# A graph kernel's last unit: one-hot rows kept in its gather buffer, and its late sums shared between VectorE and GpSimd

## The chip, the cores and the metric

The kernel runs on one core of one Trainium2 chip. The metric is the device time of one execution in microseconds. An execution with the profiler on takes longer than one without; times without it are the metric, and the profile tells what happens inside.

## What is computed

The input is x (4096 nodes, 64 values each) and a 0/1 adjacency matrix of 4096 x 4096 with about 8 neighbours per row. Two layers follow one another, each with a layer norm and a ReLU ahead of it and a residual sum behind it. Cut to what matters:

```
# layer 0, on h = relu(layernorm(x)), curvature 1
w      = adj / max(adj.sum(1), 1e-8)
log_ij = logmap(h_i, h_j)                 # per edge: Mobius difference, arctanh of its norm
agg    = einsum('ij,ijc->ic', w, log_ij)
x      = x + expmap(0, agg @ weight0 + bias0)     # a tanh of the norm

# layer 1, on h = relu(layernorm(x))
support = h @ weight1
rank    = cumsum(adj != 0, axis=1);  deg = rank[:, -1];  k = min(deg, 100)
w       = (adj != 0) * where(rank - (deg - k) > 0, 0.5 ** (deg - rank), 0)
out     = x + w @ support + bias1
```

## The kernel before

Rows are handled in 32 blocks of 128. Four stages overlap in time.

**Load.** `load` reads the adjacency matrix (128 DMAs of 512 KB on SyncE's queue), TensorE transposes it (L888) and ScalarE writes it as one-byte floats to four resident arrays `masks[0..3]` (L891), eight row blocks each. TensorE packs the bits into words (L917), from which VectorE finds each row's neighbours (`search`, `tail_split`, `tail_first`, `tail_second`): up to six per row in a regular list (`ell`), and the rest of all rows in tails, three slots of 128 edges per row block.

**Units.** The edges of layer 0 are worked through in 17 units. Units 0 to 15 hold the regular lists of two row blocks (12 slots of 128 edges), and units 5 to 16 also the tails of two or three row blocks (up to nine slots). Unit 16, the last, has no regular list: it holds the tails of blocks 30 and 31, six slots. A unit goes through these steps:

- `fetch`: the unit's own rows come in by DMA on ScalarE's queue. For a tail this is `hr`, placed in the second half of a tile `mr` from the pool `blk`, which has one buffer; the first half becomes `mt`.
- `gather`: one indirect DMA per slot on GpSimd's queue (L1139) fills tile `g` (pool `gp`, two buffers; 21 slots of 65 floats per partition).
- `tail_rows`: ScalarE builds one-hot rows `oh` (L1156, L1163; one buffer in `blk`), TensorE transposes them into the one-bank pool `ps_m` (L1169), ScalarE copies them to `mt` (L1170), and TensorE picks the rows of `hr` with them (L1178): the first six slots into bank `sel` of `ps_s`, the others into `ps_m`.
- `differ` (L1192 to L1222): differences of gathered and own rows to tile `d`, and their squares back into `g`; `weigh` (L1234 to L1251): the weight of each edge, small VectorE and ScalarE operations.
- `total`: the regular list is added up on VectorE. For the tail ScalarE scales the one-hot rows to `mr` (L1261), TensorE adds up by destination into a bank `sel` of `ps_s` (L1266), and `total_tail` adds that to `y` (L1295).

`d`, `w`, `oh` and `mr` have one buffer each, so these steps of one unit follow those of the unit before.

**Groups.** `middle` ends layer 0 and begins layer 1 for five groups of row blocks (8, 8, 8, 6 and 2). It has four stages: scale and subtract (L1323 to L1330), transposes and the product with weight 0 (L1302, L1345), tanh and layer norm on VectorE and ScalarE (L1353 to L1359, L698 to L711), and transposes and the product with weight 1 (L1386, L1390), whose result is split in three bf16 parts in `sup` (L1403). Group 3 (six blocks) needs units up to 15, group 4 (two blocks) needs unit 16.

**Sums.** `w @ support` is taken in four sums over source blocks: sum 0 has the 16 blocks of groups 0 and 1, sum 1 the seven that follow and belong to group 2, sum 2 six of group 3 and sum 3 three of group 4. Each sum is taken for 4 arrays p and 4 pairs n of row blocks, by `collect(c, p, n)`: 2 x (blocks) matmuls of 128x192 (L1422, with L1430 for the last source in sum 3) into one of the two banks of `ps_a`, and then the three parts are added into `acc`. There are two ways to do this:

- VectorE: one reduction out of the bank to `wsb` (L1441) and one multiply-add into `acc` (L1445);
- GpSimd, by way of ScalarE: a scaled copy to a tile of the right size (L1436) and three adds into `acc` (L1438). The tile is `mr` of `blk` for even n and `dg` of `lst` for odd n; each has one buffer.

Before, sums 1 and 2 take the second way always, sum 3 for n of 2 and 3, sum 0 never: 40 collects by GpSimd, 24 by VectorE. After each second collect of an array's last sum, `write` sends four row blocks out.

**The order of the work.** Each step is entered in a plan with a due time, written out by hand as `at(time, step, ...)` (L1456 and on). Steps are issued in the order of due times, and a priority is made of the due time, 30 us less for the steps named in EARLY (`fetch`, `gather`, `tail_rows`, `differ`, `weigh`, `total`, `middle` and the list steps, but not `collect`). A planner then fixes one order of instructions for each engine, and on the chip each engine runs its order, waiting at each instruction. A tile whose buffer is in use waits until all users of the buffer are done.

At the end a flag (L1559 to L1565) decides whether a general path is needed (L1567 to L1569); with these inputs it is not.

Of the kernel before, what the change touches and what calls it, by code (L numbers as in the profile page):

```python
# [11 lines left out]
F32 = mybir.dt.float32  # L12
BF16 = mybir.dt.bfloat16
# [6 lines left out]
P = 128  # L20
# [36 lines left out]
TB = 3  # L57
MAXT = 3
# [490 lines left out]
def kernel(  # L549
# [34 lines left out]
    nc = tc.nc  # L584
# [4 lines left out]
    DT = D + 1  # L589
# [4 lines left out]
    NSL = 2 * ELL + MAXT * TB  # L594
# [14 lines left out]
    hp_d = dram.tile([P, NB, 3 * DT], BF16, name="hp_d")  # L609
# [6 lines left out]
    with ExitStack() as fast:  # L616
# [174 lines left out]
        late = masks[NQ - 1].bitcast(F32).rearrange("p b c -> p (b c)")  # L791
# [39 lines left out]
        gp = fast.enter_context(tc.tile_pool(name="gp", bufs=2))  # L831
# [24 lines left out]
        for c, (_, nb, _) in enumerate(sums):  # L856
            n = nb + (c == len(sums) - 1)
# [254 lines left out]
        def fetch(u):  # L1112
            rb = u["ell"]
            if rb is not None:
                hi = blk2.tile([P, 2, DT], F32, name="hi")
                u["hi"] = hi[:, :, 1:DT]
                nc.scalar.dma_start(out=hi, in_=tab_v[:, rb : rb + 2, :])
            if u["tail"]:
                t0, nt = u["tail"]

                u["mr"] = blk.tile([P, MAXT * TB, P], F32, name="mr")
                half = u["mr"].rearrange("p b c -> p (b c)").bitcast(BF16)
                u["mt"] = half[:, 0 : MAXT * TB * P].rearrange("p (b c) -> p b c", c=P)
                hr = half[:, MAXT * TB * P :][:, 0 : MAXT * 3 * DT]
                u["hr"] = hr = hr.rearrange("p (b c) -> p b c", c=3 * DT)
                nc.scalar.dma_start(out=hr[:, 0:nt, :], in_=hp_d[:, t0 : t0 + nt, :])

        def gather(u):
            rb = u["ell"]
            g = u["g"] = gp.tile([P, NSL, DT], F32, name="g")  # L1130
            idx = []
            if rb is not None:
                idx = [ell_i[:, rb + b, s : s + 1] for b in range(2) for s in range(ELL)]
            u["e2"] = len(idx)
            if u["tail"]:
                t0, nt = u["tail"]
                idx += [tail_i[:, t0 + b, t : t + 1] for b in range(nt) for t in range(TB)]
            for k, i in enumerate(idx):
                nc.gpsimd.indirect_dma_start(  # L1139
                    out=g[:, k, :],  # L1140
                    out_offset=None,
                    in_=tab_d,
                    in_offset=bass.IndirectOffsetOnAxis(ap=i, axis=0),
                )
            u["ns"] = len(idx)

        def tail_rows(u):

            if not u["tail"]:
                return  # L1150
            t0, nt = u["tail"]
            nb = nt * TB
            oh = u["oh"] = blk.tile([P, MAXT * TB, P], BF16, name="oh")

            for k in range(nb):
                nc.scalar.activation(  # L1156
                    oh[:, k, :],
                    row128,
                    AF.Abs,
                    bias=tail_r[:, t0 + k // TB, k % TB : k % TB + 1],  # L1160
                    scale=-1.0,
                )
            nc.scalar.activation(oh[:, 0:nb], oh[:, 0:nb], AF.Relu, bias=1.0, scale=-1.0)  # L1163
            mt, u["sel"] = u["mt"], []
            for k0 in range(0, nb, SEL):
                part = range(k0, min(k0 + SEL, nb))
                mp = ps_m.tile([P, SEL, P], BF16, name="mi")
                for k in part:
                    nc.tensor.transpose(mp[:, k - k0, :], oh[:, k, :], ident_b)  # L1169
                nc.scalar.copy(mt[:, k0 : part.stop], mp[:, 0 : len(part)])  # L1170
            for k0 in range(0, nb, SEL):
                part = range(k0, min(k0 + SEL, nb))
                pool, name = (ps_m, "mi") if k0 else (ps_s, "sel")
                sel = pool.tile([P, SEL, DT], F32, name=name)
                u["sel"].append((k0, part.stop, sel))
                for k in part:
                    for n in range(3):
                        nc.tensor.matmul(  # L1178
                            sel[:, k - k0, :],
                            lhsT=mt[:, k, :],  # L1180
                            rhs=u["hr"][:, k // TB, n * DT : n * DT + DT],
                            start=(n == 0),
                            stop=(n == 2),
                        )
# [68 lines left out]
        def total(u):  # L1253

            d, rb, ns, r = (u[k] for k in ("d", "ell", "ns", "r"))
            e2 = u["e2"]
            if u["tail"]:
                t0, nt = u["tail"]
                mr = u["mr"]
                for k in range(nt * TB):  # L1260
                    nc.scalar.activation(  # L1261
                        mr[:, k, :], u["oh"][:, k, :], AF.Copy, scale=r[:, e2 + k : e2 + k + 1]
                    )
                ag = u["ag"] = ps_s.tile([P, SEL, DT], F32, name="sel")
                for k in range(nt * TB):
                    nc.tensor.matmul(  # L1266
                        ag[:, k // TB, :], lhsT=mr[:, k, :], rhs=d[:, e2 + k, :],
                        start=(k % TB == 0), stop=(k % TB == TB - 1),
                    )
            if not e2:  # L1270
                return
            q, b = divmod(rb, QB)
            if b == 0:
                st["y", q] = yp.tile([P, QB, DT], F32, name="y")

            re = r[:, 0:e2]
            nc.vector.scalar_tensor_tensor(
                re, ell_v[:, rb : rb + 2].rearrange("p b s -> p (b s)"), 0.0, re,
                ALU.is_gt, ALU.mult,
            )  # L1280
            nc.vector.tensor_tensor(d[:, 0:e2], d[:, 0:e2], cols(re, DT), ALU.mult)
            sv = d[:, 0:e2].rearrange("p (b s) c -> p b s c", b=2)
            for dst, one, two in (
                (sv[:, :, 0:3], sv[:, :, 0:3], sv[:, :, 3:6]),
                (sv[:, :, 0:1], sv[:, :, 0:1], sv[:, :, 1:2]),
                (st["y", q][:, b : b + 2, :].unsqueeze(2), sv[:, :, 0:1], sv[:, :, 2:3]),
            ):
                nc.vector.tensor_tensor(dst, one, two, ALU.add)
# [124 lines left out]

        def collect(c, p, n):

            pool = 0 < c < len(sums) - 1 or (c == len(sums) - 1 and n >= 2)
            b0, nb, _ = sums[c]
            end = c == len(sums) - 1
            o = ps_a.tile([P, 2, 2 * P], F32, name="a_ps")
            for k in range(2):  # L1420
                for j in range(nb):
                    nc.tensor.matmul(  # L1422
                        o[:, k, 0:W3],
                        lhsT=masks[p][:, b0 + j, bass.ts(2 * n + k, P)],
                        rhs=sup[c][:, j, :],
                        start=(j == 0),
                        stop=(j == nb - 1 and not end),
                    )
                if end:
                    nc.tensor.matmul(  # L1430
                        o[:, k, 0:W3], lhsT=last, rhs=sup[c][:, nb, :], start=False, stop=True
                    )
            ab = acc[:, p * QB + 2 * n : p * QB + 2 * n + 2, :]
            if pool:
                ev = (lst if n % 2 else blk).tile([P, 2, W3], F32, name="dg" if n % 2 else "mr")
                nc.scalar.activation(ev, o[:, :, 0:W3], AF.Copy, scale=2.0**-W8_SHIFT)  # L1436
                for k in range(3):
                    nc.gpsimd.tensor_tensor(ab, ab, ev[:, :, k * D : k * D + D], ALU.add)  # L1438
                return
            red = lst.tile([P, 2, D], F32, name="wsb")  # L1440
            nc.vector.tensor_reduce(  # L1441
                red, o[:, :, 0:W3].rearrange("p k (n c) -> p k c n", n=3), AX.X, ALU.add
            )
            a = ab.rearrange("p k c -> p (k c)")
            nc.vector.scalar_tensor_tensor(  # L1445
                a, red.rearrange("p k c -> p (k c)"), 2.0**-W8_SHIFT, a, ALU.mult, ALU.add
            )
# [8 lines left out]
        def at(when, fn, *args):  # L1456
            plan.append((when, len(plan), fn, args))
# [40 lines left out]
        for n, u in enumerate(units):  # L1498
# [4 lines left out]
            e2 = 2 * ELL if u["ell"] is not None else 0  # L1503
            took = 1.26 * (e2 + (u["tail"][1] * TB if u["tail"] else 0))
            t = start + took
            at(u_fetch, fetch, u)
            at(start, gather, u)
            z = start + SH
            u_fetch = z + 3.0
            at(z, tail_rows, u)  # L1510
            at(z + 1.0, differ, u)
            at(z + 4.0, weigh, u, 0)
            at(z + 5.0, weigh, u, 1)
# [78 lines left out]
```

## Time and profile before

| | |
|---|---|
| median of 3 runs without profile | 566.61 us (565.72 to 568.6) |
| the profiled execution | 754.09 us |
| its span, first to last instruction | 752.2 us |
| mean TensorE clock granted in it | 0.668 of full |
| PE / PE weight load / DVE / ACT / POOL busy | 400.0 / 344.2 / 403.2 / 345.6 / 350.5 us |
| last gather of unit 16 starts | 633.14 us |
| last L1266 of unit 16 ends, first `mr` sum evacuated | 677.49 us |
| last cast of group 4 (L1403) starts | 712.55 us |
| last GpSimd add (L1438) ends | 738.98 us |

PE is TensorE, DVE is VectorE, ACT is ScalarE, POOL is GpSimd and SP is SyncE. A group's line gives line, engine, operation, output and input tiles, shapes and count, then busy time and mean ns, then the engine's idle time just ahead of these instructions and what released it. In a timeline line the first numbers are start and length in us, and the bracket at its end holds the idle time before it and the releaser. "issue" and "remote" or "unknown queue" are waits that the profile can't name. The profiled execution is a third longer than those of the metric; most of what the profile can't name lies in its first 610 us.

### The profile page before, as it was taken

To read this page: it belongs to the slowest core of one execution; us is meant where nothing else is said; L and a number is where in the kernel's file an instruction comes from. 1 tells how busy PE (TensorE), PEld (TensorE's weight loads), DVE (VectorE), ACT (ScalarE), POOL (GpSimd) and SP (SyncE) were. 2 spreads that over 40 slices of the span, in tenths; PEclk is the share of its full clock that TensorE was granted. 3 is DMA by queue.
4 is the path that set the end of the run, shared out by engine and by line. 5 is a ranking of instruction groups with operands and counts; after the bars stand their busy time and mean duration, and the time that the engine had idled before them with its cause. 6 is when DMAs were issued, how large, how long until landed. Compare 5 with 4: busy or idle time off the path is not lost.

```text
span 752.2 us, 11841 instructions
## 1 busy us (share of the span) xinstructions
PE 400.0 (53%) x4094; PEld 344.2 (46%) x4094; DVE 403.2 (54%) x1557; ACT 345.6 (46%) x791; POOL 350.5 (47%) x423
## 2 busy tenths in 40 slices
PE   3742465643632628636067351452274378979881
PEld 3542353532531517535054241342164168979871
DVE  7742386734880518927169463793623136764520
ACT  6742465733842529836156251343242214565430
POOL 1374606246475440562705454587274713007892
PEclk9865576755855757855556555555556669988997
DMA  8994567755963536956201111221111110000001
GB/s 310 384 323 137 192 217 245 261 168 154 343 198 94 180 95 217 322 164 191 33 17 17 29 34 23 44 38 26 30 27 33 28 15 13 14 10 1 2 22 40
DMA packets 42858, 88.23 MB, mean 117 GB/s; under 512 B 14756, under 2 KB 20388, under 8 KB 42660
## 3 DMA queue, kind: packets, MB, share of 16 engines
q1 hardware_dynamic: 21458, 72.93, 26.9%
q0 software_dynamic: 9504, 10.67, 8.1%
q10 hardware_dynamic: 11826, 3.78, 2.3%
q8 instruction: 34, 0.56, 0.3%
q14 instruction: 36, 0.29, 0.1%
HBM read 83.11 MB, written 4.24 MB: 116 GB/s over the span
## 4 chain that ended last, share of the span: by engine, by line
DVE 23%; another core or an unknown queue 22%; PE 20%; ACT 16%; issue 10%; DMA 5%; ACTq 2%; POOL 1%; DVEq 0%; SPq 0%; POOLq 0%
PE a_ps L1422 9%; ACT mask L891 7%; PE a_ps L888 3%; DVE mask L1412 3%; PE words L917 2%; DMA room<-in_adj 2%; DVE cand L981 1%; DVE tl L1095 1%; DVE tb L1093 1%; ACT oh L1156 1%; PE sel L1266 1%; POOL acc L1438 1%; DVE wsb L983 1%; DMA w_sb<-in_L_gnn_weight 1%
## 5 line engine op out<-in xcount | busy, mean ns | idle before, releaser
L1139 POOL DMA_INDIRECT g<-tab_d,ell_i x192 | 198.0, 1031 | 266.2 <-DVE d L1234 84.7
L891 ACT ACTIVATE mask<-a_ps 128x1024 fp8e5<-128x1024 bf16 x128 | 128.2, 1028 | 113.8 <-remote 84.6
L888 PE MATMUL a_ps<-ident_b,room 128*128 128x128 bf16 x1024 | 107.4, 272 | 63.6 <-ACT mask L891 37.4
L1422 PE MATMUL a_ps<-room,mask 128*128 128x192 bf16 x1024 | 109.1, 260 | 32.5 <-issue 25.9
L888 PEld LDWEIGHTS <-room 128*128 128x128 bf16 x1024 | 92.9, 158 | 69.9 <-issue 68.0
L1139 POOL DMA_INDIRECT g<-tab_d,tail_i x96 | 93.8, 977 | 50.8 <-issue 28.1
L1422 PEld LDWEIGHTS <-mask 128*128 128x128 fp8e5 x1024 | 93.1, 104 | 41.1 <-issue 39.3
L917 PEld LDWEIGHTS <-mask 128*128 128x128 fp8e5 x1024 | 49.5, 115 | 107.6 <-ACT mask L891 56.7
L917 PE MATMUL words<-pk,mask 128*128 128x64 bf16 x1024 | 61.1, 219 | 70.2 <-ACT mask L891 44.4
L981 DVE MAX8 cand<-wsb 128x8 f32<-128x256 f32 x96 | 40.5, 422 | 88.5 <-ACT wsb L928 80.8
L1266 PE MATMUL sel<-d,mr 128*128 128x65 f32 x192 | 41.3, 379 | 20.2 <-issue 16.7
L1266 PEld LDWEIGHTS sel<-d,mr 128*128 128x128 f32 x192 | 39.0, 295 | 24.9 <-issue 19.6
L1438 POOL TENSOR_TENSOR acc<-acc,dg 128x128 f32<-128x128 f32 x60 | 28.2, 469 | 36.0 <-ACT dg L1436 33.9
L1412 DVE TENSOR_TENSOR mask<-mask 128x1024 int16<-128x1024 int16 x60 | 40.7, 678 | 6.6 <-ACT q__5085 L1241 4.0
L1441 DVE TENSOR_REDUCE wsb<-a_ps 128x128 f32<-128x384 f32 x24 | 13.3, 555 | 46.0 <-remote 27.8
L1261 ACT ACTIVATE mr<-oh,r 128x128 f32<-128x128 bf16 x96 | 29.3, 389 | 18.0 <-DVE acc L1445 7.5
L1438 POOL TENSOR_TENSOR acc<-acc,mr 128x128 f32<-128x128 f32 x60 | 28.5, 475 | 14.6 <-ACT mr L1436 12.7
L1169 PE MATMUL mi<-ident_b,oh 128*128 128x128 bf16 x96 | 12.6, 283 | 38.1 <-ACT oh L1163 28.2
L904 PE MATMUL words<-gn,ones_b 1*128 1x352 bf16 x32 | 12.3, 390 | 35.1 <-ACT cn L931 20.9
L1156 ACT ACTIVATE oh<-row,tail_r 128x128 bf16<-128x128 bf16 x96 | 29.4, 389 | 3.2 <-DVE tail_r L1109 3.1
L1169 PEld LDWEIGHTS <-oh 128*128 128x128 bf16 x96 | 8.9, 128 | 41.1 <-ACT oh L1163 29.2
L1170 ACT COPY mr<-mi 128x768 bf16<-128x768 bf16 (+1 forms) x20 | 13.5, 674 | 30.6 <-PE mi L1169 12.2
(332 smaller groups left out, 775.1 us busy)
## 6 DMA issues: line engine op xcount, KB each, us to landing
room<-in_adj SPq DMA_DIRECT2D x128, 512.0 KB
g<-tab_d,ell_i POOLq DMA_INDIRECT x192
hp_d<-mask SPq DMA_DIRECT2D x1, 1560.0 KB
g<-tab_d,tail_i POOLq DMA_INDIRECT x96
mr<-hp_d ACTq DMA_DIRECT2D x8, 146.2 KB
tab_d<-mask POOLq DMA_DIRECT2D x2, 520.0 KB
hi<-tab_d ACTq DMA_DIRECT2D x16, 65.0 KB
mask<-in_x SPq DMA_DIRECT2D x2, 512.0 KB
```

Of the source, the lines that this page charges most:

```text
L888: nc.tensor.transpose(a_ps[:, k, :], upper[:, e : 2 * HC : 2 * JH], ident_b)
L891: nc.scalar.activation(masks[q][:, j0 : j0 + QB, bass.ts(b, P)], a_ps, AF.Copy, scale=2.0**-ONE, saturate=False,)
L917: nc.tensor.matmul(w, lhsT=masks[q][:, j, bass.ts(b, P)], rhs=pk, start=False, stop=True, skip_group_check=True,)
L981: nc.vector.max(out=top, in_=src)
L1139: nc.gpsimd.indirect_dma_start(out=g[:, k, :], out_offset=None, in_=tab_d, in_offset=bass.IndirectOffsetOnAxis(ap=i, axis=0),)
L1156: nc.scalar.activation(oh[:, k, :], row128, AF.Abs, bias=tail_r[:, t0 + k // TB, k % TB : k % TB + 1], scale=-1.0,)
L1169: nc.tensor.transpose(mp[:, k - k0, :], oh[:, k, :], ident_b)
L1261: nc.scalar.activation(mr[:, k, :], u["oh"][:, k, :], AF.Copy, scale=r[:, e2 + k : e2 + k + 1])
L1266: nc.tensor.matmul(ag[:, k // TB, :], lhsT=mr[:, k, :], rhs=d[:, e2 + k, :], start=(k % TB == 0), stop=(k % TB == TB - 1),)
L1412: nc.vector.tensor_tensor(m[:, :, j, :], m[:, :, j, :], m[:, :, j - 1 if j else JH - 1, :], ALU.add)
L1422: nc.tensor.matmul(o[:, k, 0:W3], lhsT=masks[p][:, b0 + j, bass.ts(2 * n + k, P)], rhs=sup[c][:, j, :], start=(j == 0), stop=(j == nb - 1 ...
L1438: nc.gpsimd.tensor_tensor(ab, ab, ev[:, :, k * D : k * D + D], ALU.add)
```

## The change

It has two parts. Both touch only the end of the kernel.

The last unit has only six of the 21 slots in its `g`. The other 15 now hold `mt`, `oh` and `hr` of that unit, so its `fetch` and `tail_rows` need neither tile `mr` nor tile `oh`; `mr` is taken only in its `total`. Its `g` is allocated in `fetch`. Its picked rows go to `ps_m` and not to the bank of `ps_s`. Its `fetch` is due 2.0 us and its `tail_rows` 4.5 us after the `tail_rows` of unit 15, where they were due 3.0 us after that and 6.0 us after the start of its own gathers.

Of sums 1, 2 and 3, the collects with odd n take the GpSimd way and those with even n the VectorE way. The tile of the GpSimd way is thereby always `dg`.

```diff
@@ fetch @@
                 t0, nt = u["tail"]
+                if rb is None:
+                    u["g"] = gp.tile([P, NSL, DT], F32, name="g")
+                    nb = nt * TB
+                    left = u["g"][:, nb:, :].rearrange("p s c -> p (s c)").bitcast(BF16)
+                    u["mt"] = left[:, 0 : nb * P].rearrange("p (b c) -> p b c", c=P)
+                    u["oh"] = left[:, nb * P : 2 * nb * P].rearrange("p (b c) -> p b c", c=P)
+                    hr = left[:, 2 * nb * P :][:, 0 : nt * 3 * DT]
+                    u["hr"] = hr = hr.rearrange("p (b c) -> p b c", c=3 * DT)
+                    nc.scalar.dma_start(out=hr, in_=hp_d[:, t0 : t0 + nt, :])
+                    return
@@ gather @@
-            g = u["g"] = gp.tile([P, NSL, DT], F32, name="g")
+            if rb is not None:
+                u["g"] = gp.tile([P, NSL, DT], F32, name="g")
+            g = u["g"]
@@ tail_rows @@
-            oh = u["oh"] = blk.tile([P, MAXT * TB, P], BF16, name="oh")
+            if u["ell"] is not None:
+                u["oh"] = blk.tile([P, MAXT * TB, P], BF16, name="oh")
+            oh = u["oh"]
...
-                pool, name = (ps_m, "mi") if k0 else (ps_s, "sel")
+                pool, name = (ps_m, "mi") if k0 or u["ell"] is None else (ps_s, "sel")
@@ total @@
-                mr = u["mr"]
+                mr = u.get("mr")
+                if mr is None:
+                    mr = blk.tile([P, MAXT * TB, P], F32, name="mr")
@@ collect @@
-            pool = 0 < c < len(sums) - 1 or (c == len(sums) - 1 and n >= 2)
+            late = c >= 1 and n % 2 == 1
...
-            if pool:
+            if late:
@@ the plan @@
-            at(u_fetch, fetch, u)
+            at(u_fetch if u["ell"] is not None else before + 2.0, fetch, u)
             at(start, gather, u)
             z = start + SH
             u_fetch = z + 3.0
-            at(z, tail_rows, u)
+            at(z if u["ell"] is not None else before + 4.5, tail_rows, u)
+            before = z
```

## The prediction

> **What bounds the kernel now.** I first read the page (span, busy slices, costliest groups), then the stretches of the last 90 us, then the order of time on GpSimd, ScalarE and TensorE there. The page says that no engine is the bound over the whole span. The change touches only the last unit and the sums after it, so the end is what counts.
>
> ```profile
> span 752.2 us, 11841 instructions
> POOL 1374606246475440562705454587274713007892
> L1438 POOL TENSOR_TENSOR acc<-acc,dg 128x128 f32<-128x128 f32 x60 | 28.2, 469 | 36.0 <-ACT dg L1436 33.9
> L1438 POOL TENSOR_TENSOR acc<-acc,mr 128x128 f32<-128x128 f32 x60 | 28.5, 475 | 14.6 <-ACT mr L1436 12.7
> L1441 DVE TENSOR_REDUCE wsb<-a_ps 128x128 f32<-128x384 f32 x24 | 13.3, 555 | 46.0 <-remote 27.8
> ```
>
> GpSimd (POOL) is empty in slices 34 and 35 and full in the last ones. Its 120 adds, three for each of 40 sums, take 56.7 us. The stretches of the end (columns: length, busy us of PE, PE weight load, DVE, ACT, POOL, then clock and DMA):
>
> ```profile
> 664.00:678.00 14.00, 9.44 (x92) 8.70 (x92) 8.49 (x49) 7.95 (x25) 1.36 (x3) 0.83 0.05 13
> 678.00:697.00 19.00, 18.95 (x177) 17.74 (x176) 8.32 (x20) 9.69 (x26) 15.55 (x33) 0.86 0.01 1
> 697.00:713.00 16.00, 13.84 (x157) 13.31 (x157) 9.80 (x38) 7.86 (x24) 13.89 (x32) 1.00 0.01 2
> 713.00:723.00 10.00, 8.24 (x95) 7.65 (x93) 0.00 (x0) 3.62 (x8) 9.45 (x23) 1.00 0.01 2
> 723.00:739.00 16.00, 12.00 (x128) 10.59 (x127) 7.07 (x16) 4.69 (x10) 13.96 (x32) 1.00 0.18 61
> ```
>
> From 697 to 739 POOL is 87 to 95% busy. VectorE does nothing from 713 to 723. Why POOL starts so late, by its order of time and ScalarE's:
>
> ```profile
> 666.70 1.52 POOL L1438 TENSOR_TENSOR acc<-acc,dg 128x128 f32<-128x128 f32 x3 [32.60 <-ACT dg L1436]
> 678.05 1.83 POOL L1438 TENSOR_TENSOR acc<-acc,mr 128x128 f32<-128x128 f32 x3 [9.84 <-ACT mr L1436]
> ...
> 677.49 0.49 ACT L1436 ACTIVATE mr<-a_ps 128x384 f32<-128x384 f32 x1 [1.35 <-PE sel L1266]
> ```
>
> The first sum that needs buffer `mr` is evacuated at 677.49, released by L1266, the last matmul of unit 16's total. `blk` holds one `mr`, and each unit with a tail keeps it from fetch to total. So 39 of the 40 POOL sums come after 677.5. And what TensorE waits for when POOL has fallen behind:
>
> ```profile
> 717.89 2.14 PE L1422 MATMUL a_ps<-room,mask 128*128 128x192 bf16 x24 [0.57 <-ACT mr L1436]
> 720.60 2.14 PE L1422 MATMUL a_ps<-room,mask 128*128 128x192 bf16 x24 [0.57 <-ACT mr L1436]
> ```
>
> Two sums every 2.71 us. Six adds follow one another there at 0.453 us, which is 2.72: POOL sets the pace. The inputs of the last sum were ready at 713 (last cast of L1403 at 712.55 to 712.95), but its first matmul ran at 723.32. Some 10 us of the end are backlog.
>
> **The Trainium skill.** PSUM — Partial Sum Buffer, The four PSUM rules: GpSimd has no access to PSUM. The trace agrees: each POOL add reads `mr` or `dg`, which ScalarE filled (L1436, 0.491 us). GPSIMD Engine Reference, Elementwise: an add costs 1.96 times VectorE's. Here 0.472 us against 0.301 for VectorE's L1445 on the same 128x128, a ratio of 1.57; the trace decides. SBUF — State Buffer, Who interferes with whom: a VectorE instruction with two SBUF inputs, or a two-port one, excludes a GpSimd instruction that reads SBUF. The trace agrees in kind: L727 took 0.17 us at 672.6 with POOL idle and 0.47 at 697.8 beside POOL's adds, and three adds took up to 1.83 us instead of 1.36.
>
> **The change, part by part.**
>
> *Sums.* The sums 1, 2 and 3 have 16 collects each. POOL had 16, 16 and 8 of them; now it has the odd ones, 24. POOL loses 16 x 3 x 0.472 = 22.7 us, ScalarE 16 x 0.491 = 7.9 us, VectorE gains 16 x (0.555 + 0.301) = 13.7 us. `mr` is used by no sum any more, so sum 1 can begin once group 2 is ready (last cast ends at 664.06) and not at 677.5.
>
> *A new wait.* All POOL sums now share one `dg` buffer, where `mr` and `dg` took turns. A relay of ScalarE 0.49, three adds 1.36 and two handovers (0.07 each, 677.98 to 678.05) is 2.0 us for each pair of collects. A pair costs TensorE 28 matmuls in sum 1 and 24 in sum 2, at 0.0845 us (66 in 5.62 less the last one's drain, about): 2.37 and 2.03 us. In sum 3 it is 16, about 1.35. So sum 1 is TensorE's, sum 2 balanced, sum 3 the relay's: 8 x 2.0 = 16 us. That is what sum 3 takes now (723 to 739), so nothing is won within it.
>
> *One-hot rows.* Unit 16's six L1156 (1.86 us), L1163 (0.84), copy L1170 (0.79), six transposes, 18 matmuls L1178 (0.7) and its `hr` DMA (97.5 KB, issued on ScalarE's queue at 663.83) go ahead of unit 15's total. They lay on the path: 661.9 to 668.6, where unit 16's L1208 waits 2.03 us for them. Now L1208 waits only for tile `d`, which unit 15's last L1266 frees near 663.8: 4.7 us earlier. The work itself fits ScalarE's gaps before (4.94 idle to 634.62, 2.21 to 650.20); without that cover it costs 3.5 us in unit 15. The DMA waits for the `g` slot of unit 14, free after L1198 at 626.43; were ScalarE to reach it at 625.4, right after unit 14's L1219, L1353 and all behind it would stand 1.2 us. Bounds 0 to 1.2; I take 0, since the chain of waits runs through TensorE there. No DMA passes POOL's queue (its gathers end at 634.1) or SP's.
>
> *The bank.* Unit 16's picked rows take `ps_m` instead of `ps_s`, which unit 15's total uses until L1295 (663.83). `ps_m` has one buffer; the flag's matmul L1562 now queues behind L1208, worth 0.1 us and off the path: its DMA was done 60 us before the end.
>
> *The sum.* Sum 1: 224 x 0.0845 = 18.9 us from 664, with some 7 us of other TensorE work between (unit 16's matmuls, group 3's transposes and products): done near 690. Group 3 ends its VectorE stage at 685.9 now and its casts at 697; earlier one-hot rows take unit 16's weighing out of its way (-4), eight even evacuations come into it (8 x 0.86, say +4, the rest in gaps), and TensorE is not held up by POOL at its transposes (-2 to -4). Sum 2 starts near 693, takes 8 x 2.1 = 16.8 and lends TensorE 3.6 us to group 4: 713. Group 4 is ready by then (713 now, and it starts 4.7 earlier). Sum 3: 16 us, to 729.5, against 739.0 now: 9.5 us won. In the runs without a profile the wins can be larger. In the profiled one TensorE was short of instructions from 585 to 608 (one or two matmuls per 2.1 us, put down to issue), which pushed sum 0 to 661 and so sum 1; without that sum 1 is done before 690, and sum 2 starts as soon as group 3 is ready, near 689, with the dg relay alone behind it: 689 + 17 + 16 = 722, 17 us won. I weight the first twice, (2 x 9.5 + 17) / 3: **12.0 us**. The profiled span would be 740.2 of 752.2, the execution 742.1 of its 754.09.
>
> How this stands to the median of 566.61: the profiled execution is 188 us longer. 22% of its chain is put down to an unknown queue and 10% to issue; little of that lies after 664 (clock 1.00 and no gathers after 697), so I carry the microseconds, not the share: 566.6 - 12.0 = **554.6**, own range 549 to 560.
>
> **Rivals.**
>
> *More (chance 0.14).* Sum 1 wholly done before unit 16's total and group 4 ready by 700. The bound is group 3, then 33 us of relay, with group 3 some 3 us earlier because fewer adds exclude VectorE: 20 us won, 547. For it: L727's 0.17 against 0.47. Against it: VectorE has 13.7 us more to do.
>
> *The relay is contended (0.13).* VectorE's L1445 has two SBUF inputs; if it holds up the adds as at 678.05 (1.83 for three), a relay is 0.49 + 1.83 + 0.14 = 2.46 us, and 16 of them from 693 end at 732.4 or, with TensorE's share, at 734: 5 us won, 561.6. Against it: each L1445 is only 0.3 us in 2.
>
> *Slower (0.10): VectorE's queue.* The order is a planner's, and an engine waits in order. If sum 2's even evacuations stand ahead of the whole second stage of group 4 on VectorE, this stage (696.9 to 707.7, 11 us) starts only when sum 2 is done, near 711. Then 711 + 11 + 5.4 (its casts) + 16.5 = 744, 5 us later than now: 571.6. It decides from a start of that stage after 706. Against it: the stage has a planned head start of 30 us over collects. For it: VectorE waited 17.43 us at one L1441 at 608.7.
>
> *The change doesn't do what it says.* If the planner starts sum 1 only after unit 16 anyway, 544 matmuls (46 us) and 7 us of other work from 677.5 end at 731: 8 us, still inside my own range.
>
> **How the numbers follow.** Forecast 0.60, more 0.14, contended 0.13, slower 0.10, something else without effect 0.03. About 0.5% (2.8 us) is what a measurement of this kernel can tell from no change. Faster by more than that: 0.60 + 0.14 + 0.08 of the contended case = 0.82; same: 0.05 + 0.03 = 0.08; slower: 0.10. The range of 546 to 565 leaves out the slower case and half of the larger gain.
>
> **What would show it.** In the changed profile: L1438 x72, all on `dg`, L1441 x40; the first evacuations of sum 1 well before unit 16's L1266, no `mr` in L1436; L1208 of unit 16 right after unit 15's L1266; in sum 2 TensorE and POOL both near full; in sum 3 pairs 2.0 us apart with TensorE waiting for ACT `dg`. I am wrong if POOL still runs without a gap for 50 us at the end, if VectorE stands at L1441 ahead of group 4's stage, or if unit 15 is later against unit 14 than 25.5 us (L1208 at 622.6 and 648.1 now).

## The result and the profile after

The kernel before took 566.85 us (median of 14 runs, 562.21 to 570.61), the kernel after 569.67 us (14 runs, 566.5 to 572.55). The ratio is 1.0064, with a 95% interval of 1.0039 to 1.0089: slower by 0.64%, some 3.6 us, where 554.6 had been forecast. The level changed between sets of runs whatever the kernel (the kernel before took 566 to 567 us in three sets and 755 to 765 in two, and its profile in the prediction is of the upper level), so ratios are taken within a set, and places in the profile are counted from a common zero near the end. It is the level and not the profiler that makes the profiled execution of the prediction a third longer: another profiled execution of the kernel before took 565.51 us. The ratios leave out runs more than 1.5% above the fastest of the same kernel, and in the set of the rows part alone, the sums part alone and sum 1 held these were 17 of 43 runs of the kernel before, since its fastest took only 558.46 us: with all runs the three ratios are 1.0008, 0.9960 and 1.0121.

That zero is unit 15's last difference, the L1223 that reads `mi` (L1208 before). Of the 188.5 us between the spans of the two levels, 187.3 lie ahead of it (zero at 650.45 and at 463.18). Behind it the two profiles of the kernel before agree: the last add on GpSimd ends 88.5 us after zero in the profile of the prediction, and 88.2 in one of the lower level. I call that lower one "before" from here on. Its lines, and those of the profile after, have the same numbers; L1438 of the prediction is now L1455, L1436 is L1453, L1441 is L1458, L1208 is L1223.

The page of the kernel after:

```profile
span 570.7 us, 11793 instructions
...
POOL 1138771727887775476767677877777730432560
...
L1455 POOL TENSOR_TENSOR acc<-acc,dg 128x128 f32<-128x128 f32 x72 | 34.2, 475 | 60.8 <-ACT dg L1453 57.0
L1458 DVE TENSOR_REDUCE wsb<-a_ps 128x128 f32<-128x384 f32 x40 | 22.1, 553 | 17.6 <-PE a_ps L1447 9.3
```

The counts are as predicted: 72 adds, all on `dg`, and 40 reductions. But GpSimd (POOL) is far from full at the end. The same row of the kernel before:

```profile
POOL 1138772737887776377767677877777760297981
```

In slices 35 to 38, counted from 0, it was 70 to 90% busy before and is 20 to 60% busy after. The stretches of the end after (length, busy us of PE, PE weight load, DVE, ACT, POOL, then clock, DMA share and GB/s):

```profile
478.00:492.00 14.00, 14.00 (x140) 13.00 (x140) 8.00 (x33) 5.96 (x19) 2.97 (x7) 0.92 0.02 6
492.00:502.00 10.00, 9.80 (x112) 9.23 (x112) 9.69 (x37) 2.36 (x7) 5.43 (x12) 1.00 0.01 2
502.00:508.00 6.00, 2.60 (x29) 2.37 (x29) 4.50 (x14) 1.81 (x5) 3.14 (x6) 0.97 0.01 1
508.00:522.00 14.00, 12.88 (x66) 10.65 (x66) 4.66 (x26) 4.87 (x16) 0.00 (x0) 0.52 0.01 2
...
538.00:558.00 20.00, 11.99 (x130) 10.57 (x127) 6.94 (x17) 4.42 (x9) 13.11 (x28) 1.00 0.14 48
```

From 478 to 502 TensorE (the first busy column) is full. From 508 to 522 GpSimd does nothing at all. Three lines of the order of time after say what GpSimd and TensorE wait for:

```profile
522.36 1.56 POOL L1455 TENSOR_TENSOR acc<-acc,dg 128x128 f32<-128x128 f32 x3 [14.96 <-ACT dg L1453]
540.68 0.49 ACT L1453 ACTIVATE dg<-a_ps 128x384 f32<-128x384 f32 x1 [1.63 <-POOL acc L1455]
541.22 0.41 PE L1439 MATMUL a_ps<-room,mask 128*128 128x192 bf16 x3 [0.64 <-ACT dg L1453]
```

GpSimd waits 14.96 us for the first evacuation of sum 2. In sum 3 the relay over the one buffer `dg` runs as foreseen: ScalarE waits for GpSimd to have read it, TensorE for ScalarE to have emptied the bank. The end is no longer set by GpSimd's work alone. It is the chain that makes sum 2 ready (group 2, unit 15's total, group 3), and then two sums at the relay's pace. All kernels, in us after zero, from one profile of each; the column before the ratio counts the last add from unit 14's last difference instead:

| kernel | group 2's transposes (stage 3) | unit 15's total | group 3's stage 2 | group 4's stage 2 | last add ends | the same, from unit 14 | ratio to before, 95% interval |
|---|---|---|---|---|---|---|---|
| before | -0.9 | 13.4 | 21.3 | 46.6 | 88.2 | 115.3 | 1 |
| after | 4.0 | 15.6 | 30.6 | 54.9 | 95.3 | 120.9 | 1.0064 (1.0039 to 1.0089) |
| after, second set | 4.0 | 16.2 | 32.1 | 56.0 | 97.2 | 123.4 | 1.0063 (1.0037 to 1.0090) |
| rows part alone | 4.0 | 15.6 | 28.6 | 52.1 | 91.4 | 117.0 | 1.0034 (1.0011 to 1.0056) |
| sums part alone | -0.9 | 13.4 | 23.1 | 45.9 | 85.6 | 112.8 | 1.0001 (0.9967 to 1.0036) |
| after, sum 1 held | 4.0 | 15.0 | 24.4 | 52.1 | 98.1 | 124.1 | 1.0130 (1.0084 to 1.0177) |
| after, rows step due as before | 4.0 | 16.1 | 30.1 | 55.9 | 95.8 | 121.8 | 1.0046 (1.0025 to 1.0066) |
| after, rows step held in its old place | -0.9 | 13.4 | 22.9 | 45.1 | 85.5 | 113.6 | 0.9964 (0.9943 to 0.9985) |
| rows part alone, held | -0.9 | 13.4 | 23.4 | 46.6 | 86.6 | 113.7 | 0.9973 (0.9950 to 0.9996) |
| after, unused matmuls | 4.0 | 15.6 | 30.4 | 52.6 | 94.0 | 120.9 | 1.0056 (1.0033 to 1.0080) |
| after, two relay buffers | 4.0 | 15.2 | 30.6 | 54.7 | 88.8 | 115.9 | 0.9965 (0.9941 to 0.9988) |
| after, rows held and two buffers | -0.9 | 13.4 | 23.0 | 45.2 | 79.1 | 107.0 | 0.9858 (0.9809 to 0.9908) |
| sums part and two buffers | -0.9 | 13.4 | 23.1 | 45.8 | 79.4 | 107.3 | 0.9887 (0.9843 to 0.9930) |

The first column alone parts the runs in two: 4.0 wherever unit 16's one-hot rows could start early, -0.9 wherever they could not. The zero itself moves a little with it. Counted from unit 14's last difference (436.06 before, 437.17 after), behind which group 2's stage 2 begins 2.6 us later in every profile, zero comes at 27.1 before and at 25.6 after. The lines of the table with 4.0 so show up to 1.5 us more delay than there is: from unit 14 the last add of the kernel after is some 5.5 us late and not 7.1, unit 15's total 0.7 and not 2.2, group 3's stage 2 7.7 and not 9.3.

### The profile page after: what moved, and what is told of

It is laid out like the page before. It is cut to its first block, busy times and chain, and to the rows that moved or that the text cites. A ratio compares the mean times of both kernels' runs of the same rounds, so it can differ in the third digit from the quotient of the medians.

```text
span 570.7 us, 11793 instructions
## 1 busy us (share of the span) xinstructions
PE 385.2 (67%) x4094; PEld 335.0 (59%) x4094; DVE 411.0 (72%) x1589; ACT 336.2 (59%) x775; POOL 340.6 (60%) x375
## 4 chain that ended last, share of the span: by engine, by line
POOL 32%; DMA 15%; DVE 15%; PE 15%; issue 12%; ACT 7%; ACTq 1%; SPq 0%; DVEq 0%; POOLq 0%
POOL g L1152 29%; PE a_ps L1439 7%; DMA g<-tab_d,ell_i 5%; DMA g<-tab_d,tail_i 4%; POOL acc L1455 3%; DMA room<-in_adj 3%; ACT mask L891 2%; DVE mask L1429 2%; DMA tab_d<-mask 2%; PE sel L1283 2%; PE a_ps L888 1%; ACT dg L1453 1%; DVE d L1249 1%; PE t L1403 1%; PE o L1319 1%
## 5 line engine op out<-in xcount | busy, mean ns | idle before, releaser
L1152 POOL DMA_INDIRECT g<-tab_d,ell_i x192 | 206.5, 1075 | 106.0 <-issue 55.2
L888 PE MATMUL a_ps<-ident_b,room 128*128 128x128 bf16 x1024 | 102.5, 264 | 34.2 <-DMA room<-in_adj 20.9
L888 PEld LDWEIGHTS <-room 128*128 128x128 bf16 x1024 | 89.3, 157 | 45.6 <-issue 43.5
L1439 PE MATMUL a_ps<-room,mask 128*128 128x192 bf16 x1024 | 103.5, 256 | 10.4 <-ACT dg L1453 5.1
L1455 POOL TENSOR_TENSOR acc<-acc,dg 128x128 f32<-128x128 f32 x72 | 34.2, 475 | 60.8 <-ACT dg L1453 57.0
L981 DVE MAX8 cand<-wsb 128x8 f32<-128x256 f32 x96 | 40.3, 420 | 15.8 <-ACT wsb L928 15.2
L1283 PE MATMUL sel<-d,mr 128*128 128x65 f32 x192 | 38.7, 362 | 16.2 <-ACT mr L1278 16.2
L1458 DVE TENSOR_REDUCE wsb<-a_ps 128x128 f32<-128x384 f32 x40 | 22.1, 553 | 17.6 <-PE a_ps L1447 9.3
L1278 ACT ACTIVATE mr<-oh,r 128x128 f32<-128x128 bf16 x90 | 27.6, 389 | 9.9 <-DVE r L1266 8.8
L1237 ACT ACTIVATE g<-d 128x1344 f32<-128x1344 f32 (+3 forms) x17 | 19.1, 1122 | 22.2 <-DVE d L1207 9.1
L1453 ACT ACTIVATE dg<-a_ps 128x384 f32<-128x384 f32 x24 | 11.7, 489 | 33.1 <-POOL acc L1455 18.4
L1171 ACT ACTIVATE oh<-row,tail_r 128x128 bf16<-128x128 bf16 x90 | 27.6, 390 | 4.4 <-DVE tail_r L1109 4.3
L983 DVE MATCH_REPLACE8 wsb<-cand,wsb 128x256 f32<-128x256 f32 x64 | 26.2, 410 | 0.0
L1249 DVE TENSOR_REDUCE d<-g 128x21 f32<-128x1344 f32 (+3 forms) x17 | 21.7, 1277 | 5.5 <-ACT g L1237 5.4
```

The costliest lines, as they stand in the source:

```text
L888: nc.tensor.transpose(a_ps[:, k, :], upper[:, e : 2 * HC : 2 * JH], ident_b)
L981: nc.vector.max(out=top, in_=src)
L1152: nc.gpsimd.indirect_dma_start(out=g[:, k, :], out_offset=None, in_=tab_d, in_offset=bass.IndirectOffsetOnAxis(ap=i, axis=0),)
L1171: nc.scalar.activation(oh[:, k, :], row128, AF.Abs, bias=tail_r[:, t0 + k // TB, k % TB : k % TB + 1], scale=-1.0,)
L1249: nc.vector.tensor_reduce(d2, u["g"][:, 0:ns, 1:DT], AX.X, ALU.add)
L1278: nc.scalar.activation(mr[:, k, :], u["oh"][:, k, :], AF.Copy, scale=r[:, e2 + k : e2 + k + 1])
```

## The experiments

**The kernel before, at the level of the kernel after.**

> The kernel before, unchanged, for a second profile of it whose TensorE clock can be set beside that of the kernel after. All theories: 567, plus or minus 4. The order theory (sum 1's matmuls, no longer held back by mr, stand ahead of group 3's transposes and product in TensorE's queue, and group 3, group 4 and sum 3 come later) expects group 3's stage 2 on VectorE to begin some 8 us after unit 15's total (15 in the kernel after), and GpSimd to work with hardly a gap for the last 50 us. The clock theory (TensorE runs out of work during group 3's stage 2 and then runs on a halved clock) expects no stretch of clock near 0.5 here between the last gather and the last sum.

565.51 us. Group 3's stage 2 begins 8.0 us after unit 15's total (13.4 to 21.3 in the table), in the kernel after 15.0. The clock was at 0.50 here too, from 484.7 to 495.0, which the clock theory had ruled out. So far this fits the order theory; it doesn't say what made the order.

**The two parts, each alone.** Rows alone is the kernel after with the choice of `collect` as before:

```diff
-            late = c >= 1 and n % 2 == 1
+            late = 0 < c < len(sums) - 1 or (c == len(sums) - 1 and n >= 2)
```

Sums alone is the kernel before with

```diff
-            pool = 0 < c < len(sums) - 1 or (c == len(sums) - 1 and n >= 2)
+            pool = c >= 1 and n % 2 == 1
```

> Only the rows part: the last unit's one-hot rows in its gather buffer, the sums evacuated as before. Order theory: sum 1 is freed from mr here too and gets ahead of group 3 on TensorE, but its evacuations alternate between mr and dg on GpSimd; mr is still free until the last unit's total, so GpSimd starts earlier; 560 to 568, group 3's stage 2 late as in the kernel after, hidden in part by GpSimd's work. If the rows part is itself the loss (rival): 569 or more. If the rows part is only a gain, as the prediction held: 558 to 562.

> Only the sums part: the rows stay in mr as before, and every second evacuation of sums 1 to 3 goes to VectorE, the others over one buffer to GpSimd. Order theory: VectorE's evacuations and the ones over dg no longer wait for mr at all, so sum 1 gets ahead of group 3 here as in the kernel after, and the rows bring nothing: 568 to 575. Relay theory (the single buffer dg makes a pair 2.2 us): the same, 568 to 573. If the rows part is the loss (rival): 555 to 562.

Rows alone: 566.5 against 566.04 us, ratio 1.0034. Sums alone: 563.78 us, ratio 1.0001 (intervals here and below in the table); its last add is 2.6 us earlier than before, so a small gain is likely and not shown. The order theory as I first had it falls here. With the sums part alone, sum 1 is just as free of `mr`, yet group 3's stage 2 begins at 23.1 and not at 30.6. With the rows part alone it begins at 28.6. The delay of the chain comes with the rows; the sums part adds some 2 us to it (28.6 to 30.6, 21.3 to 23.1).

**Sum 1 held behind group 3's stage 1 on TensorE.** The cure that the first theory asked for, with sum 1's due times 8 us later:

```diff
+                    with ExitStack() as es:
+                        if c == 1:
+                            es.enter_context(tc.issue_after(st["s1", 3].ins))
                         nc.tensor.matmul(
```

> The kernel after, with sum 1's matmuls queued on TensorE behind group 3's transposes and product (its stage 1), and nothing else changed. Order theory: group 3's stage 2 begins 5 to 7 us earlier, sum 2 and sum 3 follow as much earlier: 556 to 563. Clock theory: TensorE has sum 1's matmuls to do during group 3's stage 2, so that the clock stays near 1.00: 565 by this alone, and lower together with the order. Relay theory or the rows as the loss: 567 to 571.

572.87 us, ratio 1.013: worse than the kernel after. Group 3's stage 2 did come 6.2 us earlier (24.4), but GpSimd's first add of sum 1 came at 30.9 instead of 21.7, sum 1's matmuls then stood among group 3's stage 3, and its last collect, put behind group 4 by the later due times, waited for group 4's stage 2, whose own addition to `acc` ends at 521.86. In the order of time on GpSimd (L1458 is L1455 of the kernel after):

```profile
522.01 1.64 POOL L1458 TENSOR_TENSOR acc<-acc,dg 128x128 f32<-128x128 f32 x3 [9.35 <-DVE ln_mean L699]
```

That wait is the edit's own, so the run neither confirms nor refutes the first theory. It shows that of the 6.2 us at group 3 only 2.8 were left at group 4's stage 2 (52.1 instead of 54.9).

**Where the rows get in the way.** The instruction orders of the two kernels are the same until group 2's stage 2. The first line in which they part is ScalarE's: one of the six L1171. The tanh of group 2's stage 2 in the order of time before (L717, L718 on ScalarE, then L720 on VectorE):

```profile
445.86 0.21 ACT L717 ACTIVATE th_r<-vn 128x8 f32<-128x8 f32 x1 [6.60 <-DVE vn L716]
446.10 0.21 ACT L718 ACTIVATE th_r<-th_r 128x8 f32<-128x8 f32 x1
446.57 0.16 DVE L720 TENSOR_TENSOR th_n<-vn,th_r 128x8 f32<-128x8 f32 x1
```

and after:

```profile
440.87 1.86 ACT L1171 ACTIVATE g<-row,tail_r 128x128 bf16<-128x128 bf16 x6 [0.51 <-DVE d L1249]
446.91 0.21 ACT L717 ACTIVATE th_r<-vn 128x8 f32<-128x8 f32 x1 [4.17 <-DVE vn L716]
448.03 0.22 ACT L1256 ACTIVATE q__6301<-q__6301 128x21 f32<-128x21 f32 x1 [0.91 <-DVE q__6301 L1255]
448.16 0.83 ACT L1178 ACTIVATE g<-g 128x768 bf16<-128x768 bf16 x1
448.89 0.19 ACT L718 ACTIVATE th_r<-th_r 128x8 f32<-128x8 f32 x1
449.11 0.17 DVE L720 TENSOR_TENSOR th_n<-vn,th_r 128x8 f32<-128x8 f32 x1
```

The rows need only `tail_r` and a free gather buffer, so the planner starts the six L1171 as soon as ScalarE is free, and their L1178 lands between the two halves of group 2's tanh, behind an L1256 that waits for VectorE. From L717 to L720 it is 2.20 us instead of 0.71. The Trainium skill (PSUM — Partial Sum Buffer, Engine vs sequencer instructions) says that ScalarE's queue is strictly first in, first out; these lines agree: L718 had its input at 447.12 and ran at 448.89, behind an L1256 that waited for VectorE until 448.03 and behind L1178. In the kernel before L718 stands ahead of L1256. So about half of the delay is L1178's own time and half is the place behind L1256.

A delay of 1.5 us is not 7.7. The rest comes with the order that the planner makes of it. Group 2's last step (L711) and unit 15's differences before:

```profile
460.32 0.69 DVE L711 SCALAR_TENSOR_TENSOR y<-y,ln_r 128x512 f32<-128x512 f32 x1
...
462.29 0.60 PE L1319 MATMUL o<-ident,y 128*64 128x128 f32 x4
463.18 0.35 DVE L1223 TENSOR_TENSOR d<-g,mi 128x192 f32<-128x192 f32 x1 [0.84 <-PE mi L1193]
```

and after:

```profile
462.73 0.35 DVE L1223 TENSOR_TENSOR d<-g,mi 128x192 f32<-128x192 f32 x1 [0.48 <-PE mi L1193]
464.44 0.68 DVE L711 SCALAR_TENSOR_TENSOR y<-y,ln_r 128x512 f32<-128x512 f32 x1
466.74 0.60 PE L1319 MATMUL o<-ident,y 128*64 128x128 f32 x4
```

Group 2 now ends behind unit 15's differences. Its transposes (L1319) stand on TensorE behind all of unit 15's second picks, 47 matmuls of sum 0 and unit 16's six transposes; before they stood right behind the first of those picks. Group 2's stage 3, unit 15's total and group 3's stage 1 are one row of TensorE work from there, and with each step further matmuls of sums 0 and 1 get ahead: between unit 15's total and group 3's first transposes stand 46 in the kernel after and 22 in the one with the sums part alone. So the new theory: **the place of six one-hot rows on ScalarE**, not the buffer that they are kept in. One edge (an order between two instructions that the planner has to keep) tests it, the rows step due as before and queued behind unit 15's weighted rows, where it stood:

```diff
-            at(z if u["ell"] is not None else before + 4.5, tail_rows, u)
+            at(z, tail_rows, u)
...
+                with ExitStack() as es:
+                    if u["ell"] is None:
+                        es.enter_context(tc.issue_after(st["mr"].ins))
                     nc.scalar.activation(
```

(`st["mr"]` is the last L1278 of the unit before; lines behind the edit have numbers 3 higher.)

> The kernel after, unchanged, beside the others of this call. All theories: 1.003 to 1.010 of the kernel before, about 569 to 570.

> The kernel after, with unit 16's one-hot rows on ScalarE queued behind unit 15's weighted rows, where they stood before the change; they still go to the gather buffer. Order theory in its new form (the six rows, free to start early, are put ahead of group 2's tanh on ScalarE; group 2's stage 3, unit 15's total and group 3's stages follow late, with sum 0's and sum 1's matmuls ahead of them on TensorE): as fast as the sums part alone, 562 to 565, with group 3's stage 2 beginning 22 to 24 us after unit 15's last difference instead of 30.6. If the rows cost by where they are stored or read, or by GpSimd's relay: 568 to 571.

769.72 us for the kernel after and 763.3 with the edge, against 764.52 before: ratios 1.0063 and 0.9964, intervals apart. Every place in the table goes back to that of the sums part alone, within 0.8 us. In the order of time with the edge, the tanh is whole again:

```profile
640.69 0.21 ACT L717 ACTIVATE th_r<-vn 128x8 f32<-128x8 f32 x1 [1.46 <-DVE vn L716]
640.93 0.21 ACT L718 ACTIVATE th_r<-th_r 128x8 f32<-128x8 f32 x1
641.27 0.16 DVE L720 TENSOR_TENSOR th_n<-vn,th_r 128x8 f32<-128x8 f32 x1
```

In the kernel after of the same set L718 starts 0.95 us behind L717 and not 0.24, again behind L1256 and L1178; L720 starts 7.27 us behind L717, because it now also stands on VectorE behind an L1458 that waits 6.17 us.

**The due time without the edge.** Only the first line pair of the diff above.

> The kernel after, with the due time of unit 16's rows step as before the change, but without the edge that holds it: the planner still puts the six one-hot rows ahead of group 2's tanh on ScalarE (they are free to start), while unit 16's transposes and selection on TensorE go back behind unit 15's total. Order theory: both places cost, so about half of the loss is left: group 2's stage 3 late as in the kernel after, group 3's stage 2 begins 25 to 28 us after unit 15's last difference (30.6 after, 23 with the edge), 0.998 to 1.003 of before. If only TensorE's share of the rows step matters: 0.996, as with the edge. If only the six rows on ScalarE matter: 1.005 or more.

570.01 against 567.29 us, ratio 1.0046. I had expected half of the loss to go, since unit 16's transposes and selection do fall back behind unit 15's total. None of it went: group 2's transposes at 4.0, group 3's stage 2 at 30.1. The six rows on ScalarE, with the order that the planner makes from there, are enough by themselves.

**The rows part alone, held by the same edge.**

> The rows part alone with the rows step held in its old place by the edge, the sums evacuated as before. Order theory: 1.000 of before, plus or minus 0.003: the loss of the rows part (1.0034) is gone, and it gains nothing, since GpSimd, which evacuates all of sums 1 and 2, then waits for group 3's sums and sets the end. If freeing mr is a gain of its own (the prediction's first term): 0.990 to 0.995.

565.43 against 567.29 us, ratio 0.9973: with the loss gone the rows part gains 0.3%, a little more than I expected of it and far less than the prediction's first term would have. GpSimd starts at 15.3 instead of 16.2 and gets ahead with sum 1, but then waits 7.0 us (until 513.25) for the first evacuation of sum 2, and with 40 sums in all it still ends at 86.6.

**The relay.** Two buffers in turn in sums 2 and 3, where `mr` is free again:

```diff
-                ev = (lst if n % 2 else blk).tile([P, 2, W3], F32, name="dg" if n % 2 else "mr")
+                ev = (lst if n == 1 or c == 1 else blk).tile([P, 2, W3], F32, name="dg" if n == 1 or c == 1 else "mr")
```

> The kernel after, with two relay buffers in turn in sums 2 and 3. Relay theory (each pair of node sums costs GpSimd 2.2 us where its three adds take 1.5): sum 3 takes 8 times 0.5 to 0.6 us less, and sum 2 nothing, since TensorE itself needs 2.15 us for two of its pairs: 564 to 566. If the order alone sets the end: 568 to 571.

762.79 against 764.52 us, ratio 0.9965, that is 0.9% or 7 us below the kernel after of the same set, where 4 to 5 were expected. Sum 3 with two buffers, in the order of time:

```profile
737.69 0.49 ACT L1453 ACTIVATE dg<-a_ps 128x384 f32<-128x384 f32 x1 [0.99 <-PE a_ps L1447]
738.25 1.52 POOL L1455 TENSOR_TENSOR acc<-acc,dg 128x128 f32<-128x128 f32 x3
739.17 0.49 ACT L1453 ACTIVATE mr<-a_ps 128x384 f32<-128x384 f32 x1 [0.99 <-PE a_ps L1447]
739.73 1.52 POOL L1455 TENSOR_TENSOR acc<-acc,mr 128x128 f32<-128x128 f32 x3
```

A pair takes 1.48 us, and ScalarE waits for TensorE and no more for GpSimd. In the kernel after a pair of sum 3 takes 2.18 (evacuations from 540.68 to 555.97, seven steps). Eight times 0.70 is 5.6. Sum 2 gains too: 17.2 us (717.50 to 734.73) instead of 18.9 (521.79 to 540.68).

**The clock.** TensorE has nothing to do from 505.2 to 507.9 and then runs at clock 0.50. 32 unused matmuls during group 3's stage 2 fill that pause:

```diff
+                    fill = ps_m.tile([P, W3], F32, name="mi")
+                    half = hx[m % 2][0][:, 0 : nb * D].bitcast(BF16)
+                    for _ in range(32):
+                        nc.tensor.matmul(fill, lhsT=ident_b, rhs=half[:, 1 : 2 * W3 : 2], start=True, stop=True)
```

> The kernel after, with 32 unused matmuls that keep TensorE at work during group 3's stage 2. Clock theory: no stretch at 0.50 between 505 and 522; group 3's stage 3 and group 4's stage 1 take 7.7 us instead of 9.8, so 2 to 3 us less: 566.5 to 568. If the clock costs nothing there or falls all the same: 569 to 571.

769.63 us, ratio 1.0056, the same as the kernel after within the intervals. The stretches with the filling (group 3's stage 3 begins at 703.9, group 4's stage 2 at 711.64):

```profile
705.00:707.00 2.00, 1.72 (x15) 1.65 (x15) 0.00 (x0) 0.53 (x2) 0.00 (x0) 1.00 0.04 8
707.00:709.00 2.00, 1.54 (x8) 0.90 (x7) 0.85 (x2) 1.48 (x4) 0.00 (x0) 0.60 0.00 0
709.00:711.00 2.00, 2.00 (x11) 2.00 (x10) 0.28 (x1) 0.87 (x3) 0.00 (x0) 0.50 0.01 4
```

The clock falls all the same, some 3.5 us later in the same work. Group 4's stage 2 is 2.3 us earlier (52.6), but the last add only 1.3 (94.0 against 95.3). In sums alone and in the run with the edge the clock falls there too, but not for as long. From zero to the last add TensorE is at 0.50 for 17.1 us in the kernel after (3.4 from 476.9 and 13.7 from 507.65), for 6.8 in each of the five kernels whose rows start late, and for 10.2 in the kernel before. At 0.50 the pairs of 64x64 products (L1403, L1407) follow one another at 0.43 us instead of 0.22, so half of the 10.3 us between the kernel after and the five, some 5 us, is my estimate of the most that the clock can hold of the delay. With the unused matmuls the two stretches are 3.4 and 10.2. So the pause during group 3's stage 2 is not what makes the clock fall, but the halved clock is not cleared: it goes with the late order in every run, and no run parts the two.

**Both cures, and the sums part with two buffers.**

> The kernel after with unit 16's one-hot rows queued where they stood before the change, and two relay buffers in turn in sums 2 and 3. Order theory and relay theory together: group 4's stage 2 begins 45 us after unit 15's last difference (56 in the kernel after), sum 2 goes at TensorE's 2.15 us for two pairs and sum 3 at 1.6: GpSimd ends 79 to 80 us after that difference, where the kernel before ends at 88: 7 to 9 us faster than before. If two gains don't add up because VectorE or ScalarE then sets the end: 2 to 4 us faster than before.

> The kernel before with the sums part of the change and two relay buffers in turn in sums 2 and 3; the last unit's rows stay in mr. Order theory: the rows in the gather buffer bring nothing once their place on ScalarE is that of before, so as fast as the run with both, within 2 us: 7 to 9 us faster than before. If storing the rows in the gather buffer is a gain of its own: 3 us or more slower than the run with both.

747.85 and 747.03 against 755.22 us, ratios 0.9858 and 0.9887; the last add ends at 79.1 and 79.4, as expected for both. They are faster than both kernels of this study, by 1.4 and 1.1% than the kernel before. With six runs of each no difference between them shows, so the rows in the gather buffer bring nothing that can be seen once they are out of the way.

## Why the prediction was wrong

The step that failed is the pricing of the **one-hot rows**: "The work itself fits ScalarE's gaps before (4.94 idle to 634.62, 2.21 to 650.20); without that cover it costs 3.5 us in unit 15." I looked for its cost in unit 15. It fell on group 2, which the prediction doesn't mention as touched. The six L1171 do fit a gap (1.86 us from 440.87). What follows them doesn't: L1178, 0.83 us, and an L1256 ahead of it stand within group 2's tanh (1.5 us late), and the order made from there brings group 3's stage 2 at 30.6 instead of 21.3, or 7.7 us late counted from unit 14. How much of this is the order itself and how much the clock that goes with it stays open.

Point by point:

- *Counts, bank, `mr`.* Right: 72 and 40, no `mr` in L1453, first evacuation of sum 1 at 483.88 before unit 16's total at 491.5.
- *Unit 16's differences earlier.* Right in itself: L1223 at 478.60, directly behind unit 15's total at 478.33. That they take "unit 16's weighing out of its way" (-4) was wrong: the weighing moved from group 3's stage 2 to stage 0 and 1, and this stage takes 14.5 us (493.33 to 507.8), no less than before (14.1).
- *Sum 2 starts near 693*, 42.5 us after zero. Measured 54.5 (517.19) in the kernel after and 44.7 with the edge. Of the 12.0 us that the kernel after is late, 9.8 are the rows' place and 2.2 an optimism about group 3; counted from unit 14 they are 7.3 and 3.0 of 10.2. "Group 4 is ready by then" held, as late as everything else: its last cast ends at 536.54, ahead of sum 3's first matmul at 537.98.
- *The relay, 2.0 us a pair.* The right mechanism, mis-sized: 2.18. The three adds take 1.52 and not 1.36, beside VectorE's work. Sums 2 and 3, from sum 2's first matmul to the last add, took 40.9 us and not 36.5. And "nothing is won within" sum 3 was accepted too easily: a second buffer was worth 6.4 us (85.5 to 79.1).
- *The warning sign* "unit 15 later against unit 14 than 25.5 us" did not show (436.56 to 461.35, 24.8). It was put on the differences, which came earlier; what came late was group 2 (its transposes by 3.3 us, counted from unit 14) and hardly unit 15's total (0.7).
- *Rivals.* Slower by VectorE's queue did not happen: group 4's stage 2 begins at 517.66, ahead of sum 2's first evacuation. The contended relay holds in part (2.18 of its 2.46). The larger gain did not come either: sum 1 was not done before unit 16's total. None of the rivals named the rows' place on ScalarE.

Taken together, in the place of the last add: freeing GpSimd of 16 sums is worth 9.1 us (88.2 to 79.1), near the 9.5 of the prediction's sum, if the rows stay in place and the relay keeps two buffers. The change gives 6.4 of it back by sharing one relay buffer and 9.8 by starting six rows early (79.1, 85.5, 95.3). Counted from unit 14 the three are 8.3, 6.6 and 7.3. That the first comes near the forecast is in part luck, since the prediction counted on one relay buffer for it and on a group 3 earlier than in any run.

What stays open: the last add comes some 5.5 us later in the pair of profiles counted from unit 14 (7.1 from zero), the medians differ by 2.8 to 5.2. The profiled executions of the kernel after are the slowest of their sets (572.55 of 566.5 to 572.55). Single executions of one kernel and set differ by 6 us and more, so I can't say from these whether a little is won ahead of zero.

## What to carry to other kernels

When a change takes away a wait, ask not only what starts earlier but in front of whom: here six instructions that could start early were put into the first gap, and on an engine that works in order what came behind them delayed a short chain that passes there. If a step has no hurry, keep it behind something with an edge; a later due time alone did not do it here. And look at a relay over one buffer: each handover is in the way of the next sum, and a second buffer brought 1.48 us a pair instead of 2.18.

## What was not expected of the hardware

TensorE's clock stayed at 0.50 far longer than the pause that went before. In the kernel after it paused 2.7 us, and these two stretches, among others, follow:

```profile
508.00:510.00 2.00, 1.33 (x6) 0.81 (x6) 0.00 (x0) 0.88 (x2) 0.00 (x0) 0.50 0.00 0
518.00:520.00 2.00, 2.00 (x13) 1.51 (x11) 1.72 (x15) 0.57 (x4) 0.00 (x0) 0.50 0.00 0
```

It is at 0.50 from 508 to 520, with TensorE busy for 11 of the 12 us, and back at 1.00 from 522. The Trainium skill (TensorE: Matmul & The Clock Gate, What's actually happening) has full rate return after about 3.4 us of sustained work. Here TensorE worked without a break from 514.43, on 64x64 float32 products and from 517.19 on mostly on the 128x192 bf16 matmuls of sum 2, and full rate came back at 521.3, 6.9 us later. Nor does a fall need a pause. Earlier in the same profile TensorE worked without a break (3.00 us of 3.00), and its clock fell to 0.50 at 476.9:

```profile
471.00:474.00 3.00, 3.00 (x33) 2.67 (x31) 2.96 (x8) 2.78 (x9) 0.00 (x0) 1.00 0.00 0
474.00:477.00 3.00, 3.00 (x28) 2.93 (x27) 0.99 (x4) 1.90 (x7) 0.00 (x0) 0.99 0.00 0
477.00:480.00 3.00, 3.00 (x19) 2.85 (x19) 1.93 (x7) 1.18 (x5) 0.00 (x0) 0.50 0.09 22
```

From 473.8 to 477.6 it ran float32 products alone there, and full rate was back at 480.3, behind bf16 matmuls. That it is the kind of work that counts is suggested by this and not shown, since no run changed it.
